# A two-layer SCNN on one core: x kept by channel and half, first weights placed by TensorE, first coefficients in PSUM, products for four rows, and a column scan fed from SBUF

## The chip, the core and the metric

The kernel runs on one core of a Trainium2 chip. The core has TensorE (PE: matrix products into PSUM), VectorE (DVE), ScalarE (ACT), GpSimd (POOL) and SyncE (SP), which mostly issues DMAs. SP, ScalarE and GpSimd each have a queue of DMAs. The metric is the device time of one execution in microseconds (us), as the median of several runs.

## The reference

x has the shape (32 images, 48 channels, 64 rows, 128 columns) in float32. Two layers, each with its own weights:

```python
x = x + _L0_conv_ref(_gn(x), ...)
x = x + _L1_conv_ref(_gn(x), ...)

# _gn: groupnorm, 16 groups of 3 channels; mean and variance per image and group
# inside _Ln_conv_ref; conv is a 1D convolution, 48 channels to 48, 5 taps
D[0] = x[0];   D[h] = x[h] + conv(D[h-1], down_w) + down_b      # rows, downwards
U[63] = D[63]; U[h] = D'[h] + conv(U[h+1], down_w) + down_b     # rows, upwards, same weights
R[0] = U[0];   R[v] = U[v] + conv(R[v-1], right_w) + right_b    # columns, to the right
L[127] = R[127]; L[v] = R[v] + conv(L[v+1], left_w) + left_b    # columns, to the left
```

The upward scan adds D of the row above the one that it makes (D' is D shifted by one row, the last one D[63]). Every row and every column depends on the one before it, so a layer has 2 x 63 row steps and 2 x 127 column steps in sequence. A row's convolution runs over its width, a column's over its height.

## The kernel before

**Phases.** The 32 images are four groups of 8. Twelve phases run one after the other (the table PHASES): a "rows" phase scans one group in one layer down and up (126 steps), a "cols" phase scans a pair of groups (two "halves") right and left (254 steps). The order is rows x0, rows x1, columns of this pair, rows x2, rows of layer 1's group 0, rows x3, columns of the second pair, rows of layer 1's groups 1 to 3, and the two column phases of layer 1. Two column phases (numbers 2 and 6 of the list, which starts at 0) come directly after the rows phase of their own second group; `follows` names them. They are called seams below.

**A step** (`step`, matmul L741, VectorE's scalar_tensor_tensor L750) makes one row or column. Channels and eight neighbouring positions lie on 3 x 128 partitions: 8 x 48 = 384, in three blocks, by the table PIECES (ten pieces: position e, channels c0 to c1, block o, first partition p0). The five taps with all neighbours become nine 128 x 128 x 128 float32 products (PRODUCTS), in the trace 18 matmul records, and three VectorE instructions add product, bias and the old row. In a rows phase the eight positions are e = w % 8, in a columns phase h % 8.

**SBUF.** One `arena` holds three slots and four stage units. A row image fills two slots, h below 32 in one, the rest in the other. A pair in column layout needs four quarters (`quarter`, 32 columns each, a slot each, so one is spilled to DRAM). `early` holds the weights down0, down1 and right (unused weight space serves as scratch at the start), then `last` and `junk`.

**DRAM copies.** `source[0]` (xin) is x in an order suited to both layouts: for each channel column position e, quarter, row and 32 values (4 columns of 8 images, "128-byte runs"). `source[1]` (mid) is the first layer's result, `ups` the result of the rows phases. `by_row`, `lines` and `by_col` are views of such a tensor: one for rows in row layout, one for rows as the input has them, one for columns.

**Input path.** `take_in` (L553) loads rows of x for the 8 images, partitions (channel, s) with s = 0 for h below 32 and 1 above. `permute` (L560, copies at L569) reorders one row pair (r and 32 + r) by four copies, `put_out` (L571) writes it to xin with two DMAs, one for each s, `move_rows` (L589) brings rows from DRAM into row layout by ten DMAs for eight rows, `scale_rows` (L606, ScalarE, L614) or `scale_at_once` (L618, L625) normalizes. The coefficients come from `scaling` (L312): an average over groups by a small product (L322), an expansion to row layout (L333), and a chain of small instructions on VectorE (L354 to L401; the groups' key is x0, x1, x2, x3, r0 to r3). With slack 0 they run on VectorE, otherwise partly on GpSimd.

**Order.** `at(t, fn, ...)` puts work on an agenda, t in steps; before each step everything due is emitted. `in_order` ties every instruction to the one before it on its engine, so each engine and DMA queue runs in program order.

**The start** (`first_group`, emitted as a whole ahead of the first step) handles group 0. It loads the x of 8 images in 16 DMAs (first all images' rows of `parts[0]`: r 0 to 15 with both s, then `parts[1]`: r 16 to 31) on SP. On ScalarE's queue `load_weights("down0")` copies the taps to DRAM and from there into the banded weight layout (5 + 25 DMAs), `load_constants` the masks and biases (2 + 10). VectorE takes the statistics (`InputStats`, L422, L425). `rows_by_product` makes rows 0 to 3 and 4 to 7 in row layout directly by TensorE products with identity pieces `to_row` (`make_ident`, L1074) and copies of PSUM by ScalarE (L1081), everything else goes through xin. Rows 0 to 3 are scaled by VectorE at once, the others in pieces of eight by ScalarE.

**A seam before.** The rows phase writes its rows to `upa` in pieces of eight, the last (first in h) in pieces of six and two; GpSimd's queue loads what the first quarter needs from there (`load_unit`, a a block of eight rows, e a row in it). `hold_queues` (L648) keeps SP's and ScalarE's next loads behind by a DMA to `pin` and a copy, each of which reads the second column of the first quarter; then follow the loads of quarter 1, alternating between SP and ScalarE.

Of the kernel before, what the change touches and what calls it, by code (L numbers as in the profile page):

```python
# [29 lines left out]
F32 = mybir.dt.float32  # L30
# [90 lines left out]
def kernel(  # L121
# [72 lines left out]
    source = [kept("xin"), kept("mid")]  # L194
# [9 lines left out]
    pin = dram.tile([FULL, 1], F32, tag="pin", name="pin")  # L204
# [9 lines left out]
    def by_row(t, e, h0, h1):  # L214


        t = t.rearrange("c (i q a e n) -> e a c i q n", i=E8, q=NQ, a=NH, e=E8)[e, h0 // E8]
        return t[:, h0 % E8 : h0 % E8 + h1 - h0].rearrange("c i q n -> c (i q) n")

    def lines(t, h0, h1):  # L220

        t = t.rearrange("c (i q a n) -> a c i q n", i=E8, q=NQ, a=NH)[h0 // E8]
        return t[:, h0 % E8 : h0 % E8 + h1 - h0].rearrange("c i q n -> c (i q) n")
# [9 lines left out]
    tail = {}  # L233

    def in_order(fn, *args):
# [5 lines left out]
        for ins in traced[n:]:  # L241
            if ins.engine in tail:
# [7 lines left out]
                )  # L250
            tail[ins.engine] = ins
# [29 lines left out]
    def load_constants(dma):  # L281
        for s in range(2):
            dma(sided(mask_sb)[s], mask[SIDES[s], SIDES[0]])
        for e, c0, c1, o, p0 in PIECES:
            dma(bd[p0 : p0 + c1 - c0, o], bias[c0:c1])
# [25 lines left out]
    def scaling(key, layer, g, averages, masks, slack=0):  # L311
# [5 lines left out]
        pool = nc.gpsimd if slack else nc.vector  # L317
# [25 lines left out]
        mean = small("mean")  # L343
        spare = small("dev")
        dev = spare[0 : FULL if n > 1 else PX, 0:n]
        if n > 1:
# [3 lines left out]
            expand(ps[:, 1 : 1 + NG], mean_c)  # L350
            yield
            nc.vector.tensor_tensor(dev, mean_p, ps[:, 1 : 1 + NG], ALU.subtract)
        else:
            nc.vector.tensor_tensor(dev, mean_p, ps[0:PX, 0:1], ALU.subtract)  # L354
        if n > 1:
            nc.vector.tensor_copy(mean, ps[:, 1 : 1 + NG])
# [6 lines left out]
        if n == 1:  # L363
            expand(ps[:, 2 + NG :], dev[:, 0])
        else:
# [5 lines left out]
            expand(ps[:, 2 + NG :], var_c)  # L371
        yield
        var = small("var")
        nc.vector.tensor_scalar(var, ps[:, 2 + NG :], GN_EPS, None, ALU.add)

        std = small("std")
        nc.scalar.activation(std, var, AF.Sqrt)
        if n == 1:
            expand(ps[:, 1 : 1 + NG], mean_p[:, 0])
        yield  # L380
        if n == 1:
            nc.vector.tensor_copy(mean, ps[:, 1 : 1 + NG])
        yield
        for _ in range(slack):
# [4 lines left out]
        pool.tensor_tensor(t0, var, r0, ALU.mult)  # L389
# [3 lines left out]
        scale, offset = (  # L393
            stat_pool.tile(
                [FULL, NG, GB], F32, tag=f"{t}{layer}{g}", name=f"{t}{layer}{g}"
            )
            for t in ("scale", "offset")
        )
        pool.tensor_tensor(scale, r0, t0, ALU.mult)
        pool.tensor_tensor(offset, mean, scale, ALU.mult)  # L400
        pool.tensor_scalar(offset, offset, -1.0, None, ALU.mult)  # L401
        coeffs[layer, g] = scale, offset
# [168 lines left out]
    def put_out(g, r, perm):  # L571


        n = perm.shape[-1] // (W * GB)
        for s in range(2):
            h = s * HALF + r
            dma(
                lines(source[0][g], h, h + n),
                sided(perm)[s].rearrange("p (m n) -> p m n", n=LINE),
            )  # L580
# [8 lines left out]
    def move_rows(k, h0, h1, to_dram):  # L589
# [4 lines left out]
        for h in range(h0, h1, E8):  # L594
            end = min(h1, h + E8)
            for o in range(NG):
                for e, c0, c1, p0 in pieces(o):
                    here = view[p0 : p0 + c1 - c0, o, h % HALF : h % HALF + end - h]
                    here = here.rearrange("p h (q n) -> p (h q) n", q=NQ)
                    there = by_row(t, e, h, end)[c0:c1]  # L600
# [25 lines left out]


# [20 lines left out]
    def hold_queues(k):  # L648

        done = quarter(k, 0)[:, 0, 0, RUN : RUN + 1]  # L650
        dma(pin, done)
        nc.scalar.copy(junk[:, BN - 1 :], done)
# [10 lines left out]
    def load_residual(k, j, i, nat):  # L663
# [3 lines left out]
        for e, c0, c1, p0 in pieces(o):  # L667
            dma(nat[p0 : p0 + c1 - c0], by_col(t, e, j)[c0:c1], nc.scalar if layer else None)
# [184 lines left out]
    def plan_rows(k, t0, prev):  # L853
# [13 lines left out]
        if following and follows(k + 1):  # L867
            cuts = [0, E8 // 4] + cuts[1:]
# [19 lines left out]
    def plan_cols(k, t0, prev):  # L888
# [3 lines left out]
        if follows(k):  # L892
            at(t0 + 1.2, hold_queues, k)
        for i in range(n):
            if follows(k) and UNITS[i][1] == 1:
# [4 lines left out]
                at(t0 - 1.5, load_unit, k, 0, i, 0, 1, E8 // 4, E8, other)  # L900
                at(t0, load_unit, k, 0, i, 0, 1, 0, E8 // 4, other)
# [3 lines left out]
            if follows(k):  # L905
                queue = nc.scalar if i % 2 else nc.sync
# [117 lines left out]
    def first_group():  # L1024
# [7 lines left out]

        def make_ident():
            for m, (e, c0, c1, o, p0) in zip(to_row, PIECES):
# [11 lines left out]
        rows = HALF // 2  # L1046
        parts = [wide_nat(SLOT + i * 2 * HALF * N * 2, rows) for i in range(2)]
        stats = InputStats("x0", GB)
        n = W * GB
# [10 lines left out]
        def permute_rows(i, r0, r1, ring, *engines):  # L1060
            for r in range(r0, r1):
                permute(parts[i], r, ring[r % len(ring)], engines)

        def put_rows(i, r0, r1, ring):
            for r in range(r0, r1):
                put_out(0, i * rows + r, ring[r % len(ring)])
# [18 lines left out]

        for i in range(2):
            for b in range(GB):
                take_in(0, i * rows, parts[i], slice(b, b + 1))
        nc.vector.memset(spare["right"], 0.0)
        nc.vector.memset(spare["left"], 0.0)  # L1090
        load_weights("down0", 0, DOWN, aside)
        load_constants(aside)
        make_ident()
        for b in range(GB):
            stats.take(0, parts[0], b)
        permute_rows(0, 8, 12, free, nc.gpsimd, nc.scalar)
        put_rows(0, 8, 12, free)
        rows_by_product(0, 4)
        spread_masks()
        permute_rows(0, 12, 15, free, nc.gpsimd, nc.scalar)  # L1100
        put_rows(0, 12, 15, free)
# [107 lines left out]
```

## Time and profile before

| what | us |
|---|---|
| median of 3 runs | 4292.32 (4289.52 to 4297.63) |
| profiled execution, device time | 4290.3 |
| its span, first to last instruction | 4288.2 |
| eight rows phases, 8 x 126 steps | 63 upward steps took 124.59 (from 526.61) |
| four columns phases, 4 x 254 steps | 127 leftward steps took 248.45 (from 2193.80) |
| last step to the end | from 4207.7 to 4288.2 |

The span is what the page and the trace count in; the device time lies 2.1 us above it. Times in the views are counted from the first instruction. A row of a timeline is: start, duration, engine, line, operation, what is written and what read, shape, count, and in brackets the idle time before it with what ended it. "PEld" is TensorE's loading of weights, which runs beside its products. A line name such as step_01u is the step's PSUM tile: layer 0, group 1, up. DMAs all have line L231, a helper's, and are told apart by what they write and read.

### The profile page before, as it was taken

What the parts mean: (1) busy time and instruction counts of PE and PEld (TensorE: products, weight loads), DVE (VectorE), ACT (ScalarE), POOL (GpSimd) and SP (SyncE); (2) the same over time, 40 slices, a digit from 0 to 9 for tenths busy, and PEclk for the clock granted to TensorE, in tenths of its full rate; (3) what the DMA queues carried; (4) which work ended last, traced back from release to release, by engine and by line L of the source; (5) the groups of instructions that cost most, each with busy time, mean ns of one, the idle gap of its engine ahead of it and who ended that gap; (6) DMA issues with size and microseconds to landing.
All of it is one profiled execution on the core that took longest, in us unless ns stands there. A gap on an engine that the chain in (4) does not pass through costs nothing. (4 is left out here: it accounts for less than half of the span.)

```text
span 4288.2 us, 89979 instructions
## 1 busy us (share of the span) xinstructions
PE 4058.9 (95%) x36648; PEld 4029.3 (94%) x36648; DVE 2164.5 (50%) x6503; ACT 1340.1 (31%) x2662; POOL 886.2 (21%) x906
## 2 busy tenths in 40 slices
PE   3699998999999999998999999999999999999992
PEld 1699998999999999998999999999999999999992
DVE  6345444446664444444446654444444444444443
ACT  1584301435793564100006772613000002210122
POOL 4271001325323020010005310000000024510352
PEclk9899999999999999999999999999999999999996
DMA  9599799857998979679308979939289049999999
GB/s 213 113 216 162 105 167 168 245 127 213 230 198 156 163 140 160 103 127 206 85 1 242 222 154 149 148 50 161 43 140 200 1 78 247 247 243 156 180 202 182
DMA packets 2116733, 680.12 MB, mean 159 GB/s; under 512 B 2005440, under 2 KB 2056160, under 8 KB 2076384
## 3 DMA queue, kind: packets, MB, share of 16 engines
q1 hardware_dynamic: 2015904, 581.64, 70.2%
q10 hardware_dynamic: 97216, 86.44, 9.9%
q0 software_dynamic: 3200, 6.30, 0.5%
q8 instruction: 288, 4.72, 0.5%
q14 instruction: 125, 1.02, 0.1%
HBM read 397.38 MB, written 295.98 MB: 162 GB/s over the span
## 5 line engine op out<-in xcount | busy, mean ns | idle before, releaser
L614 ACT ACTIVATE arena<-arena,offset,scale 128x256 f32<-128x256 f32 (+2 forms) x816 | 575.6, 801 | 432.9 <-DMA arena<-mid 176.1
L673 POOL TENSOR_TENSOR arena<-arena 128x2048 f32<-128x2048 f32 x80 | 363.1, 4553 | 1386.0 <-PE step_10l L741 434.1
L569 POOL COPY arena<-arena 96x256 f32<-96x256 f32 x448 | 265.0, 650 | 553.8 <-DMA arena<-in_x 444.2
L512 ACT ACTIVATE early<-arena 128x256 f32<-128x256 f32 x192 | 129.4, 674 | 477.2 <-POOL arena L673 471.2
L741 PE MATMUL step_00r<-arena,early 128*128 128x128 f32 x2286 | 251.5, 274 | 14.1 <-DMA arena<-upa 14.1
L741 PEld LDWEIGHTS step_00r<-arena,early 128*128 128x128 f32 x2286 | 251.1, 185 | 14.5 <-issue 14.4
L741 PE MATMUL step_01r<-arena,early 128*128 128x128 f32 x2286 | 250.6, 273 | 14.4 <-DMA arena<-upa 14.4
L741 PEld LDWEIGHTS step_01r<-arena,early 128*128 128x128 f32 x2286 | 250.4, 185 | 14.6 <-issue 14.5
L741 PE MATMUL step_11r<-arena,early 128*128 128x128 f32 x2286 | 251.3, 273 | 8.2 <-DVE arena L750 8.2
L741 PEld LDWEIGHTS step_11r<-arena,early 128*128 128x128 f32 x2286 | 250.8, 185 | 8.7 <-DVE arena L750 8.6
L741 PE MATMUL step_00l<-arena,wleft 128*128 128x128 f32 x2286 | 249.1, 272 | 0.0
L741 PEld LDWEIGHTS step_00l<-arena,wleft 128*128 128x128 f32 x2286 | 248.6, 184 | 0.0
L741 PE MATMUL step_10l<-arena,wleft 128*128 128x128 f32 x2286 | 248.5, 272 | 0.0
L741 PE MATMUL step_11l<-arena,wleft 128*128 128x128 f32 x2286 | 248.5, 272 | 0.0
L741 PE MATMUL step_01l<-arena,wleft 128*128 128x128 f32 x2286 | 248.4, 272 | 0.0
L741 PE MATMUL step_10r<-arena,early 128*128 128x128 f32 x2286 | 248.4, 272 | 0.0
L741 PEld LDWEIGHTS step_10l<-arena,wleft 128*128 128x128 f32 x2286 | 248.4, 184 | 0.0
L741 PEld LDWEIGHTS step_11l<-arena,wleft 128*128 128x128 f32 x2286 | 248.4, 184 | 0.0
L741 PEld LDWEIGHTS step_01l<-arena,wleft 128*128 128x128 f32 x2286 | 248.4, 184 | 0.0
L741 PEld LDWEIGHTS step_10r<-arena,early 128*128 128x128 f32 x2286 | 248.4, 184 | 0.0
L698 ACT COPY arena<-arena 128x256 f32<-128x256 f32 x172 | 99.7, 656 | 411.5 <-POOL arena L673 162.2
L240 ACT COPY early<-arena 128x1 f32<-128x1 f32 x2 | 0.4, 191 | 657.9 <-DVE arena L750 657.9
(189 smaller groups left out, 7171.3 us busy)
## 6 DMA issues: line engine op xcount, KB each, us to landing
arena<-in_x SPq DMA_DIRECT2D x24, 1536.0 KB, 11.6
xin<-arena SPq DMA_DIRECT2D x96, 384.0 KB, 4.7
arena<-xin SPq DMA_DIRECT2D x96, 384.0 KB, 8.5
mid<-arena SPq DMA_DIRECT2D x96, 384.0 KB, 7.8
arena<-mid SPq DMA_DIRECT2D x192, 192.0 KB, 4.2
upb<-arena SPq DMA_DIRECT2D x192, 192.0 KB, 3.9
arena<-upb SPq DMA_DIRECT2D x96, 384.0 KB, 12.3
arena<-xin SPq DMA_DIRECT2D x186, 192.0 KB, 4.3
```

The source lines that it names most:

```text
L240: fn(*args)
L512: nc.scalar.activation(junk[:, 0:n], view[:, b], AF.Identity, accum_out=self.sum[:, i, j : j + 1])
L569: copy(dst[:, r, q], src[:, r0 + r, q])
L614: nc.scalar.activation(args[0], args[0], AF.Identity, bias=args[2], scale=args[1])
L673: eng.tensor_tensor(unit, unit, nat, ALU.add)
L698: copy(by_w(perm)[:, a], src[:, a])
L741: nc.tensor.matmul(part(whole(ps[o])[0:m], -s), weights[:, i, at : at + m], part(src(i), s), start=seen[o] == 1, stop=seen[o] == left[o],)
```

## The change

- **x in DRAM.** Each group's xin is one tensor of 96 partitions (channel, s) with half the rows each. `put_out` is one DMA of all 96 partitions. The views are `x_by_row`, `x_by_col` and a changed `lines`; the residual loads of layer 0 read two runs of 4 KB where they read one of 8 KB.
- **First weights.** `load_kernel` fetches the five taps and the bias with six DMAs, on SP and ScalarE's queue alternately; `place_kernel` spreads them with 37 products of the identity pieces, into PSUM, and six ScalarE copies. `load_constants` shrinks to `load_masks` (2 DMAs). ScalarE's square root table is loaded at the start by a dummy instruction.
- **First coefficients.** With slack 0 (x0, x1, x3) `scaling` keeps variance, mean and one difference in the PSUM tile, so that its two-tensor instructions read one operand from PSUM.
- **Products make four rows.** `rows_by_product(4, 4)` is gone; rows 4 to 7 go through xin. `put_rows` now permutes and writes row by row, one engine for a row. `scale_first` scales rows 0 to 3 image by image: 15 VectorE instructions and 9 ScalarE instructions on 128 x 64 in place of four VectorE instructions.
- **Seams.** `send_row` copies the columns of quarter 0 in the first block of eight rows directly from row layout in SBUF to column layout in SBUF, in runs of 32 values: for e 0 to 3 row by row as the scan makes rows 7 to 0 (47 DMAs), then `send_rest` for e 4 to 7 (47), alternating between ScalarE's queue and SP. Rows 0 to 15 go to `upa` by quarters (`move_rows` with q): quarter 0 of rows 8 to 15 eight steps before the end, the others after it. GpSimd's loads of rows 0 to 7 are gone. `hold_queue` keeps only the ScalarE copy, without the DMA to `pin`; quarter 1 is loaded for half 1 on SP and half 0 on ScalarE's queue.

```diff
+    source = [
+        [
+            dram.tile([PX, MOIETY], F32, tag=f"xin{g}", name=f"xin{g}")[:, 0 : CHANNEL // 2]
+            for g in range(NGRP)
+        ],
+        kept("mid"),
+    ]
...
+    def x_by_row(t, e, h0, h1):
+        s, h = divmod(h0, HALF)
+        t = t.rearrange("(c s) (i q a e n) -> s e a c i q n", s=2, i=E8, q=NQ, a=NH // 2, e=E8)
+        t = t[s, e, h // E8, :, h % E8 : h % E8 + h1 - h0]
+        return t.rearrange("c i q n -> c (i q) n")
+
+    def x_by_col(t, e, j):
+        return t.rearrange("(c s) (i q n) -> i q c s n", s=2, i=E8, q=NQ)[e, j]
...
+            if ins.engine in queues and "DMA" in ins.opcode:
+                if fn in together and "queue" in tail:
...
+                        reason="together",
+                    )
+                tail["queue"] = ins
...
+        if not slack:
+            far = ps[0:PX, 1 + NG : 2 + NG]
+            nc.vector.tensor_tensor(far, mean_p, ps[0:PX, 0:1], ALU.subtract)
+            nc.vector.tensor_tensor(dev, mean_p, ps[0:PX, 0:1], ALU.subtract)
+            nc.vector.tensor_tensor(far, far, dev, ALU.mult)
+            nc.vector.tensor_tensor(dev, far, var_p, ALU.add)
+            yield
+            expand(var, dev[:, 0])
+            yield
+            nc.vector.tensor_scalar(var, var, GN_EPS, None, ALU.add)
+            r0 = small("std")
+            nc.scalar.activation(r0, var, AF.Sqrt)
+            expand(mean, mean_p[:, 0])
+            yield
+            yield
+            nc.vector.reciprocal(r0, r0)
+            nc.vector.tensor_tensor(var, var, r0, ALU.mult)
+            nc.vector.tensor_tensor(var, var, r0, ALU.mult)
+            nc.vector.tensor_scalar(var, var, -0.5, 1.5, ALU.mult, ALU.add)
+            nc.vector.tensor_tensor(scale, var, r0, ALU.mult)
+            nc.vector.tensor_tensor(offset, mean, scale, ALU.mult)
+            nc.vector.tensor_scalar(offset, offset, -1.0, None, ALU.mult)
+            return
...
-        for s in range(2):
-            h = s * HALF + r
-            dma(
-                lines(source[0][g], h, h + n),
-                sided(perm)[s].rearrange("p (m n) -> p m n", n=LINE),
-            )
+        dma(lines(source[0][g], r, r + n), perm.rearrange("p (m n) -> p m n", n=LINE))
...
+    def scale_first(k, h1, split):
...
+        for b in range(GB):
+            for o in range(NG):
+                it = view[:, o, b]
+                by, on = scale[:, o, b : b + 1], offset[:, o, b : b + 1]
+                if b < split:
+                    nc.vector.tensor_scalar(it, it, by, on, ALU.mult, ALU.add)
+                else:
+                    nc.scalar.activation(it, it, AF.Identity, bias=on, scale=by)
...
-    def hold_queues(k):
-        done = quarter(k, 0)[:, 0, 0, RUN : RUN + 1]
-        dma(pin, done)
-        nc.scalar.copy(junk[:, BN - 1 :], done)
+    def send_row(k, h, wanted):
+        here = row(k - 1, h)
+        for e, c0, c1, o, p0 in PIECES:
+            if e not in wanted:
+                continue
+            for i, d0, d1, to, q0 in PIECES:
+                a, b = max(c0, d0), min(c1, d1)
+                if i != h or a >= b:
+                    continue
+                turns[0] += 1
+                dma(
+                    quarter(k, 0)[q0 + a - d0 : q0 + b - d0, 1, to, e * RUN : (e + 1) * RUN],
+                    here[p0 + a - c0 : p0 + b - c0, o, 0:RUN],
+                    nc.scalar if turns[0] % 2 else nc.sync,
+                )
+
+    def send_rest(k, wanted):
+        for e in wanted:
+            for h in range(E8 - 1, -1, -1):
+                send_row(k, h, (e,))
...
+    def hold_queue(k):
+        nc.scalar.copy(junk[:, BN - 1 :], quarter(k, 0)[:, 0, 0, RUN : RUN + 1])
...
-            cuts = [0, E8 // 4] + cuts[1:]
+        seam = following and follows(k + 1)
+        if seam:
+            cuts = cuts[2:]
+            end = t0 + 2 * (H - 1)
+            at(end - E8, move_rows, k, E8, 2 * E8, True, 0)
+            for h in range(E8 - 1, -1, -1):
+                at(end - h, send_row, k + 1, h, range(0, E8 // 2))
+            at(end, send_rest, k + 1, range(E8 // 2, E8))
+            for q in range(1, NQ):
+                at(end + 0.1 if q == 1 else end + 1.6, move_rows, k, 0, 2 * E8, True, q)
...
-                at(t0 - 1.5, load_unit, k, 0, i, 0, 1, E8 // 4, E8, other)
-                at(t0, load_unit, k, 0, i, 0, 1, 0, E8 // 4, other)
...
-                queue = nc.scalar if i % 2 else nc.sync
+                queue = nc.sync if UNITS[i][1] else nc.scalar
...
+        def load_kernel():
+            nc.vector.memset(kernel, 0.0)
+            for j in range(TAPS):
+                d, si = divmod(TAPS - 1 - j, 2)
+                to = sided(kernel)[0][:, j * C : (j + 1) * C]
+                dma(to, w[SIDES[si], 0, DOWN, d, SIDES[0]], nc.scalar if j % 2 else nc.sync)
+            aside(sided(kernel)[0][:, TAPS * C :], bias[0:C].rearrange("c l k -> c (l k)"))
...
+        def place_kernel():
+            for i in range(NG):
+                ps = ps_rows.tile([FULL, BN], F32, tag=f"rows{i}", name=f"rows{i}")
+                todo = [(to_row[0], zeros, slice(0, NG * FULL + 6))]
...
+                for j, (lhs, rhs, to) in enumerate(todo):
+                    nc.tensor.matmul(
+                        ps[:, to], lhs, rhs, start=j == 0, stop=j == len(todo) - 1
+                    )
+                nc.scalar.copy(wt["down0"][:, i], ps[:, 0 : NG * FULL])
+                nc.scalar.copy(
+                    bd[:, i].rearrange("p l k -> p (l k)"), ps[:, NG * FULL :][:, 0:6]
+                )
...
-        load_weights("down0", 0, DOWN, aside)
-        load_constants(aside)
+        load_kernel()
...
+        place_kernel()
+        spread_masks()
         for b in range(GB):
             stats.take(0, parts[0], b)
...
+        put_rows(0, 4, 8, free, pool, act)
         rows_by_product(0, 4)
...
+        put_rows(0, 8, 14, free, pool, act)
+        put_rows(0, 14, 16, free, pool)
+        move_rows(0, 4, 8, False)
+        move_rows(0, 8, 16, False)
         for b in range(GB):
             stats.take(NBN // 2, parts[1], b)
             stats.aggregate(b)
...
-        scale_at_once(0, 0, 1, nc.vector)
-        scale_at_once(0, 1, 4, nc.vector)
+        scale_first(0, 4, 5)
         scale_rows(0, 4, 8)
         scale_rows(0, 8, 16)
+        put_rows(1, 0, 8, free, pool)
         move_rows(0, 16, 24, False)
         scale_rows(0, 16, 24)
...
+        put_rows(1, 8, 16, late, pool)
         move_rows(0, 24, 32, False)
         scale_rows(0, 24, 32)
...
+        put_rows(0, 0, 4, later, pool)
+        move_rows(0, 32, 40, False)
         scale_rows(0, 32, 40)
+        move_rows(0, 40, 64, False)
         take_in(1, 0, nats1[0])
```

## The prediction

> **What bounds the kernel now.** I read the page first, then the waits of TensorE, then its timeline, and for each long gap the timeline of the engine that ended it.
>
> ```profile
> span 4288.2 us, 89979 instructions
> PE 4058.9 (95%) x36648; PEld 4029.3 (94%) x36648; DVE 2164.5 (50%) x6503; ACT 1340.1 (31%) x2662; POOL 886.2 (21%) x906
> PE   3699998999999999998999999999999999999992
> ```
>
> TensorE is busy 95% of the span. The third line shows where it is not: the first four slices (107 us each), a dip in slices 7 and 19, and the last slice.
>
> ```profile
> PE rows L1074 <- DMA arena<-in_x: 41.7, 1, 41.7
> PE step_00d L741 <- DVE arena L750: 31.7, 6, 14.9
> PE step_00d L741 <- DVE arena L625: 24.7, 1, 24.7
> PE step_01r L741 <- DMA arena<-upa: 14.4, 1, 14.4
> PE step_00r L741 <- DMA arena<-upa: 14.1, 1, 14.1
> ```
>
> The columns are total, count and longest. The change can reach two places: the start, and the two seams (row scan to column scan) in slices 7 and 19. The timeline of TensorE (start, us) at the start:
>
> ```profile
> 60.01 16.57 PE L1074 MATMUL rows<-arena,early 96*128 96x512 f32 x18
> 78.22 0.35 PE L322 MATMUL ps_x<-mv_x_x,mask_x 96*96 96x8 f32 x2
> 107.83 17.66 PE L741 MATMUL step_00d<-arena,early 128*128 128x128 f32 x144 [24.72 <-DVE arena L625]
> 175.60 0.79 PE L741 MATMUL step_00d<-arena,early 128*128 128x128 f32 x2 [13.62 <-DVE arena L750]
> 208.63 0.80 PE L741 MATMUL step_00d<-arena,early 128*128 128x128 f32 x2 [14.85 <-DVE arena L750]
> ```
>
> The first step begins at 107.83, and row 32 is reached at 208.63. An unhindered step is 1.978 us (63 row steps in 124.6 us), so the 31 steps to there are 61.3 us; the other 39.5 of that 100.8 us are stalls at rows 8, 24 and 32. Behind the first step stands one VectorE line:
>
> ```profile
> 83.25 0.29 DVE L387 RECIPROCAL std_x<-std_x 128x24 f32<-128x24 f32 x1
> 83.58 22.07 DVE L389 TENSOR_TENSOR dev_x<-var_x,std_x 128x24 f32<-128x24 f32 x1
> 105.68 0.18 DVE L390 TENSOR_TENSOR dev_x<-dev_x,std_x 128x24 f32<-128x24 f32 x1
> ```
>
> L389 and L390 are alike, 22.07 against 0.18 us. GpSimd's row copies run back to back from 75.72 to 105.60 in its timeline, and L389 ends as they end. Behind rows 24 and 32 stands the SP queue:
>
> ```profile
> 104.68 1.31 SPq L231 DMA_DIRECT2D xin<-wleft x2
> 140.84 3.83 SPq L231 DMA_DIRECT2D xin<-arena x6
> ```
>
> SP waits 34.8 us here for ScalarE's L614 (the scaling of rows), so put-outs and moves of the later rows all start late.
>
> **What the Trainium skill says.** (1) "SBUF — State Buffer", section "Who interferes with whom": a VectorE instruction with two SBUF inputs contends with a GpSimd instruction that reads SBUF, the loser is blocked entirely; with at most one SBUF input, outside the two-port modes, it does not contend. The trace agrees once (L389); seven other two-input instructions that met these copies waited at most 0.4 us, so it is a risk per instruction, not a price. (2) "VectorE: DVE Perf Modes", section "Why PSUM operands drop a tier": an operand in PSUM rules the two-port mode out. No instruction of before tests this against a copy. (3) "DMA: Bandwidth & Descriptors", section "Queues, rings and completion order": each engine consumes descriptors in ring order. Agrees: put-outs issued by SP from 44.74 landed only from 66.69 on, 0.5 us apart, right behind the last x load (66.29). (4) "TensorE: Matmul & The Clock Gate", section "What's actually happening": after an idle window of about 3.4 us the clock is halved, until about as much busy time. In the windows view the clock around the seam (652 to 670) is 0.55, so I add 2.4 us to each long stall.
>
> **Loads and statistics.** The 25 weight DMAs and 10 bias DMAs on ScalarE's queue (16.52 and 8.90 us) go. SP's waits up to 260 us show that its x loads stood behind them (total, count, longest):
>
> ```profile
> SPq L231 <- DMA early<-taps: 11.9, 3, 6.2
> SPq L231 <- DMA bd<-in_b: 10.0, 2, 7.7
> SPq L231 <- DMA taps<-in_w: 8.2, 1, 8.2
> ```
>
> So the first eight loads land 5 to 6 us apart, the eighth at 41.57, and the later ones 3.0 apart. Now three tap DMAs of SP stand ahead (about 0.6 us each), the first load lands at about 8, the eighth at 8 + 7 x 3.0 = 29, the sixteenth at 53 to 54 instead of 66.29. VectorE's statistics take 2.47 + 0.37 us per load, less than the gap, so they end at 57. Placing the weights by TensorE is 37 small products and six copies, before the eighth load, in TensorE's empty 41.7 us: nothing. One product instead of two (18.6 us) ends near 48, ahead of 57; before, the second held the averages to 78.22. Averages: 57.3 instead of 78.22, -21 us.
>
> **First coefficients.** From 78.22 to the last coefficient is 28.5 us, of which L389 is 22. With PSUM operands no tensor-by-tensor instruction has two SBUF inputs, so no wait of that kind is left; one more VectorE instruction is 0.2, and the PSUM tile makes the expansion wait for ScalarE's square root (0.6; the table is loaded earlier, -1.3). 28.5 - 22 = 6.5: coefficients at 64. In place of four VectorE instructions (4.1 us) come 15 VectorE (0.2 to 0.55 each; not in before at this shape, the small TENSOR_SCALAR rows are 0.17 to 0.28) and 9 ScalarE (0.395 each, 3.6 us). They are single-source in SBUF, so they may meet copies: below 3 us alone, 22 more if starved. I take 5: first step at 69.5, -38.
>
> **Rows after the first four.** Rows 4 to 7 now go through DRAM. Twelve put-outs queue behind the loads; a row is 1.0 us of transfer, so the ring of seven buffers turns over from 54; the last copies end at about 63. Then ten moves (8.7 us for eight rows, 6 to 8.7 here) and 3.1 us to land: 73 to 75. ScalarE's 24 scalings x 0.395 = 9.5 end at 83.5. The scan needs row 4 at 69.5 + 3 x 1.978 = 75.4: stall 8 + 2.4. Rows 8 to 15: 24 x 0.508 = 12.2 more, 95.7 against a need of 93.8: 2. After that each eight rows cost GpSimd 19 us of copies (2.36 a row), SP 5 of put-outs (one 0.6 us issue for a row instead of two) and 9 of moves, and ScalarE 12.2, against 15.8 of scan. Copies from 63 on end at 82 and 101 (rows 16 to 23, 24 to 31), their put-outs at 86 and 102, moves land at 98.5 and 114.5, scalings end at 110.7 and 126.7, against needs of 111.5 and 127.3. Rows 32 to 39 need only four more copies: 139 against 143. I found no wait of these put-outs for ScalarE, which removes the 34.8 us. These margins are thin: I add 4 us. Sum of stalls 16.4 against 39.5. Row 32 at 69.5 + 61.3 + 16.4 = 147.2 instead of 208.63: -61; rounded to -60, since group 1's loads must come as much earlier (SP reaches them at some 160 instead of 225.30, -65, so they do).
>
> **Seams.** A column step is 248.45 / 127 = 1.956. From the last row step to the end of the right scan there are 265.5 us at the first seam (651.2 to 916.7) and 265.0 at the second: 16.8 over 248.4. Now 94 DMAs of 128-byte runs go from SBUF to SBUF, 47 on each of the two queues: 23.5 while the last eight rows are made, 2.5 of them after the last row, and 23.5 behind. With c us per DMA on a queue, the last column of the first eight lands 0.35 + 26c + 2.0 us after the scan (small DMAs at the seam land after 1.9 to 2.5) and is needed six steps (11.7) after the first. Excess: 26c - 9.4 + 2.4 of clock, at c = 0.57 (put-out issues measure 0.55 to 0.6) 7.8. Ten moves precede on SP (6 us), which I charge 0.7. So 8.5 instead of 16.8, twice: -17. At c = 0.5 it is -20. Above c = 0.67 the queues lag behind the rows already (2.94 sends on each in 1.978 us), all 47 run from seven rows (13.8 us) before the end, and the excess becomes 47c - 20.8: at 0.8 the gain is 0. The quarter's other columns come as whole rows behind these sends, some 15 steps ahead of their use.
>
> **Rest.** x1's and x3's scaling wait for a square root, 0.6 each: +1. One put-out for two on a queue, 4 KB runs for 8 KB in the residual loads: beside an engine-bound scan, 0. The tail (80 us from 4207.7) isn't touched. Sum on the profiled run's own 4290.3 (span 4288.2): 4290.3 - 60 - 17 + 1 = 4214. The median of the runs is 2.0 above the profiled one: 4216.
>
> **The rivals.** (a) VectorE's scale instructions starve as L389 did, or the loads stay 5.7 us apart because another queue's DMAs hold the semaphores. For: L389 itself; against: 30 fewer DMAs between. Coefficients at 76 to 86 instead of 64; but rows 16 to 40 are set by SP and ScalarE with some slack, so of 12 to 22 us only 10 to 15 show: 4228. (b) The seam gives nothing (c near 0.8; weight DMAs took 16.52 / 25 = 0.66, bias DMAs 0.89): 4233. (c) The other side: the sends choke the seam, because two queues carry 94 tiny DMAs while the DMA share there is 0.95 (640 to 652). Excess 47c - 20.8 must exceed 16.8 by 30 on each seam to eat the start's gain: c above 1.43. At 1.6 it is 54, and the time 4292 + 2 x 37.6 - 59 = 4308. (d) It doesn't do what it says: a put-out still waits for ScalarE or for a buffer, and row 32 keeps its 34.8 us wait in part: row 32 at 175, 4244.
>
> **How the numbers follow.** Forecast 0.58, (a) 0.17, (b) 0.13, (d) 0.06, (c) 0.05, and 0.01 that gains and losses cancel. Forecast's own range: first step 67 to 73, stalls 12 to 20, seam -10 to -24: 4200 to 4230. To hold 8 in 10 it has to reach (a) and (b), and 4195 below for a seam that hides entirely: 4196 to 4242. A change under 0.2% (8.6 us) can't be told from none. Faster 0.94, same 0.01, slower 0.05.
>
> **What would show it.** Right: the first step near 69, a stall of about 10 at row 4 and none above 4 after it, no tensor-by-tensor instruction above 1 us before it, the sixteenth x load at 54, row 32 near 147; at each seam a first wait below 5 us, small waits within eight steps. Wrong: a VectorE scale of over 5 us, SP waiting for L614, a stall at rows 16 to 32 above 5, queue spacings above 0.8 us at a seam, or a wait of the columns on later loads.

## Result and the profile after

The changed kernel takes 4239.2 us (median of 4 runs, 4236.2 to 4246.9) against 4290.9 before (4 runs, 4278.9 to 4297.6): ratio 0.9881, 95% interval 0.9867 to 0.9895. Predicted were 4216, in a range of 4196 to 4242. So it is faster by 52 us instead of the 76 forecast: inside the stated range, near its upper end, and outside the forecast's own range of 4200 to 4230.

The profiled execution is the slowest of the four: its span is 4245.1 us, 43.1 below that of before. First the page's head with TensorE's busy tenths in 40 slices. Of the low slices of before (3 and 6 at the start, 8 in slices 7 and 19) a 6 at the start is left, and an 8 is new in slice 8, in the right scan. Then TensorE's waits (total, count, longest):

```profile
span 4245.1 us, 90421 instructions
PE   6999999899999999999999999999999999999992
```

```profile
PE step_00d L837 <- DVE arena L846: 12.4, 7, 6.6
PE step_00r L837 <- DVE arena L846: 11.2, 1, 11.2
PE step_00d L837 <- DVE arena L690: 6.9, 2, 6.5
PE step_00r L837 <- DMA arena<-arena: 6.0, 1, 6.0
PE step_01r L837 <- DMA arena<-arena: 5.8, 2, 5.0
```

Where 31.7 and 24.7 us of waiting stood at the start there are 12.4 and 6.9, and the seams' first waits are 6.0 and 5.0 instead of 14.1 and 14.4. But step_00r, the right scan behind the first seam, has a wait of 11.2 that wasn't there before. The timeline of TensorE shows where these lie; the last row of the fence is VectorE's, in the wait of 11.2:

```profile
70.83 0.77 PE L837 MATMUL step_00d<-arena,early 128*128 128x128 f32 x2 [6.53 <-DVE arena L690]
...
120.22 0.80 PE L837 MATMUL step_00d<-arena,early 128*128 128x128 f32 x2 [6.60 <-DVE arena L846]
...
605.71 16.98 PE L837 MATMUL step_00r<-arena,early 128*128 128x128 f32 x126 [6.05 <-DMA arena<-arena]
624.34 174.52 PE L837 MATMUL step_00r<-arena,early 128*128 128x128 f32 x1604 [1.65 <-DMA upa<-arena]
810.09 62.14 PE L837 MATMUL step_00r<-arena,early 128*128 128x128 f32 x556 [11.23 <-DVE arena L846]
...
809.68 0.61 DVE L846 SCALAR_TENSOR_TENSOR arena<-step_00r,bd,arena 128x128 f32<-128x128 f32 x2 [11.55 <-DMA arena<-upa]
```

The first step begins at 70.83 instead of 107.83. In step_00r, 126 + 1604 matmuls of 18 a step are 96 steps: the scan stops where quarter 3 begins, because VectorE waits for a load of it. From the first matmul of each phase in both traces:

| stage | before | after | difference |
|---|---|---|---|
| to the first step of x1 (step_01d) | 400.8 | 350.5 | -50.3 |
| first seam: upward scan x1 and right scan | 390.1 | 397.0 | +6.9 |
| second seam: upward scan x3 and right scan | 389.5 | 387.2 | -2.3 |
| step_02d, rows behind the first columns phase | 127.1 | 134.1 | +7.0 |
| all else | | | -4.4 |

Of "all else", 3.2 lie in the last right scan, step_11r. It takes 256.2 us here and 255.5 to 260.2 in the other traces, so this isn't to be put down to the change.

A seam's two scans without any wait are 124.5 + 248.3 = 372.8 us; what is above that I call its excess: 17.3 and 16.7 before, 24.2 and 14.4 after.

So the start gains 50 of the 60 us forecast, and the seams give nothing: 38.6 us of excess after, 34.0 before, 17 forecast. Two questions are left: what eats the seams' gain, and which part of the change made the start's.

### The profile page after: what moved, and what is told of

It reads as the page before. It is cut to its first block, busy times and chain, and to the rows that moved or that the text cites. A ratio compares the mean times of both kernels' runs of the same rounds, so it can differ in the third digit from the quotient of the medians.

```text
span 4245.1 us, 90421 instructions
## 1 busy us (share of the span) xinstructions
PE 4072.4 (96%) x36704; PEld 4050.5 (95%) x36704; DVE 2142.6 (50%) x6517; ACT 1346.5 (32%) x2680; POOL 870.8 (21%) x879
## 5 line engine op out<-in xcount | busy, mean ns | idle before, releaser
L837 PE MATMUL step_00r<-arena,early 128*128 128x128 f32 x2286 | 253.6, 275 | 18.9 <-DVE arena L846 11.2
```

The lines of the kernel that those rows point to most:

```text
L837: nc.tensor.matmul(part(whole(ps[o])[0:m], -s), weights[:, i, at : at + m], part(src(i), s), start=seen[o] == 1, stop=seen[o] == left[o],)
```

## Experiments

All but experiment 9 start from the changed kernel; a diff shows what differs, with "..." for lines left out. "Step 33" is the first matmul of step 33 of the first phase: 208.6 before, 160.4 after, and 157.7 to 159.5 in experiments 1 to 4, which have the same start (first step at 69.0 to 70.8). Experiments 5 to 8 and 10 are one execution each. Since executions of the changed kernel alone spread from 4236 to 4248, these five are read by their stages more than by their one time.

**1. The changed kernel again.**

> The changed kernel a second time, unaltered. In its profile the first seam's right scan stood 11.2 us at column 97, waiting for the last loads of quarter 3, which landed 203.6 us after the first column step (166.9 before the change). Theory S (SP's order: 60 moves to DRAM that used to lie ahead of the column scan now lie in SP's queue between quarter 0 and the loads of quarters 1 to 3): the loads land again near 200 us after the first column step, and a stall of 3 to 15 us is there again. Theory N (the stall belongs to that one execution, whose time was 4246.9 against 4236 to 4242 of the others): no stall, and the right scan of the first seam takes about 251 us.

4246.2 us (ratio to before 0.9885, 0.9855 to 0.9915). The stall is there again, 6.3 us at the same step:

```profile
812.19 63.14 PE L837 MATMUL step_00r<-arena,early 128*128 128x128 f32 x556 [6.33 <-DVE arena L846]
```

The excess is 23.2 at the first seam and 9.4 at the second. It isn't one execution's accident: the stall stands in all seven traces that keep these seams (the two, and experiments 5 to 8 and 10), with 3.5 to 15.0 us.

**2. The seams of before.**

```diff
-            cuts = cuts[2:]
...
-            at(end, send_rest, k + 1, range(E8 // 2, E8))
...
+            cuts = [0, E8 // 4] + cuts[1:]
...
+                at(t0 - 1.5, load_unit, k, 0, i, 0, 1, E8 // 4, E8, other)
+                at(t0, load_unit, k, 0, i, 0, 1, 0, E8 // 4, other)
```

> The changed kernel with the seams of the kernel before: rows to DRAM in pieces, GpSimd loads the first quarter, both queues held. Only the start is then changed. From the end of the row scan to the end of the right scan 265.5 us at the first seam (272.4 in the profile of the changed kernel), 265.0 at the second (262.6). My forecast of the new seams was -8.3 each, so by it this kernel is 17 us slower than the changed one. Theory S: the new seams are worth -3 to -5 each at their beginning, and +11 at column 97 of the first, so this kernel is between 8 us slower and 5 us faster.

4234.2 us (0.9864, 0.9837 to 0.9890), 12 below the changed kernel beside it. The intervals overlap, so it isn't shown to be faster, but it isn't 17 us slower, as my forecast wanted. Excess 17.9 and 17.2, no stall at quarter 3:

```profile
612.04 251.62 PE L840 MATMUL step_00r<-arena,early 128*128 128x128 f32 x2286 [14.61 <-DMA arena<-upa]
```

The old seam pays 14.6 us once and then nothing. The new one pays it in pieces. The two excesses of a kernel sum to 34 to 35 us in the three traces with the old seams (before, this one and experiment 9) and to 33 to 41 in the seven with the new ones. As a part of the change the seams are worth nothing.

**3. Moves of quarters 1 to 3 by GpSimd's queue.**

```diff
-                at(end + 0.1 if q == 1 else end + 1.6, move_rows, k, 0, 2 * E8, True, q)
+                at(end + 0.1, move_rows, k, 0, 2 * E8, True, q, nc.gpsimd)
```

> The changed kernel, but the 60 moves of quarters 1 to 3 of rows 0 to 15 to DRAM are issued by GpSimd's queue right behind the row scan, in place of SP's behind its sends. Theory S (order of SP): quarter 1's loads start 15 to 20 us earlier, quarter 3's last load lands 20 to 35 us earlier (near 170 us after the first column step), no stall at column 97, first seam 261 us, time 5 to 11 us below the changed kernel. Rival B (the 16 DMA engines are full from 625 to 800, share 0.92 to 1.04, so that it doesn't matter who issues): quarter 3 lands within 5 us of where it was, the stall stays.

4237.2 us (0.9868, 0.9845 to 0.9891), 9.0 below the changed kernel beside it (the intervals overlap). The stall at quarter 3 is gone, and the first seam's excess falls from 24.2 to 11.5:

```profile
604.22 16.40 PE L837 MATMUL step_00r<-arena,early 128*128 128x128 f32 x126 [6.79 <-DMA arena<-arena]
622.38 234.90 PE L837 MATMUL step_00r<-arena,early 128*128 128x128 f32 x2160 [1.76 <-DVE arena L846]
```

The bytes are the same, and only the issuing queue differs, with the time of the issue, so SP's order set the stall (theory S), not the DMA engines (rival B). SP's queue in the changed kernel behind the first row scan shows it (start, duration, count):

```profile
589.15 31.23 SPq L250 DMA_DIRECT2D arena<-arena  x47
620.42 15.74 SPq L250 DMA_DIRECT2D upa<-arena  x20
641.04 12.15 SPq L250 DMA_DIRECT2D arena<-upa  x10
653.24 28.55 SPq L250 DMA_DIRECT2D upa<-arena  x40
```

Before the change 30 moves of whole rows did this work, and SP had issued them by 659.6, ahead of the columns (665.3). Now sixty moves of quarters (upa<-arena) take 44 us of SP behind the sends, and the later loads on SP come late: the last of quarter 3 lands 203.6 us after the first column step instead of 166.9 (175.1 in this experiment). At the second seam it is late too, 154.6 instead of 118.3, but there that is still ahead of its use, 96 column steps or 187.8 us after the first.

The second seam's excess is 17.3 here, though: the last send on SP landed 6.0 us after its issue (mean 2.4), and the scan waited 4.4 us for it. The second seam with sends on two queues varies, from 9.4 to 17.3 in eight traces.

**4. Sends on three queues.** As experiment 3, and:

```diff
-                    nc.scalar if turns[0] % 2 else nc.sync,
+                    (nc.scalar, nc.sync, nc.gpsimd)[turns[0] % 3],
```

> As the kernel with the moves on GpSimd's queue, and the 94 sends alternate over three queues, ScalarE's, SP's and GpSimd's, 31 or 32 on each. In the changed kernel a send takes 0.64 us of a queue, the last lands 24.1 us after the row scan, and the excess of a seam over its column steps is 12.7 and 14.1 us (without the stall at column 97). If a queue's issue paces them: the last send lands 14 us after the row scan and the excess falls to 6 or 7 on each seam, 6 to 7 us less than the kernel with two queues. If the DMA engines or the landing pace them: no change. If GpSimd's sends are dearer than 1 us: the excess grows.

4220.8 us (0.9831, 0.9808 to 0.9854). Excess 6.5 and 7.0:

```profile
603.66 250.32 PE L837 MATMUL step_00r<-arena,early 128*128 128x128 f32 x2286 [4.55 <-DMA arena<-arena]
```

The last send lands 15.2 us after the row scan's end instead of 24.1. With two queues a send follows the last on its queue after 0.67 to 0.71 us, with three after 0.72 to 0.79 (behind the row scan after 0.70 to 0.74 on SP's and ScalarE's, 0.50 on GpSimd's), so 94 of them pass at 0.34 and some 0.27 us each. The queues' issue paces them, as supposed; the DMA share in the changed kernel in this stretch is at most 0.28.

**5. Coefficients in SBUF.**

```diff
-        if not slack:
+        if False:
...
-        pool = nc.gpsimd
+        pool = nc.gpsimd if slack else nc.vector
```

> The changed kernel with the coefficients of x0, x1 and x3 worked out in SBUF again, as before. Before the change one VectorE instruction of this chain (two SBUF inputs) took 22.07 us beside GpSimd's copies; now these copies run from 58.4 to 65.5 and the chain from 60.0 to 65.6. Forecast's theory (two SBUF inputs can be blocked by a GpSimd copy, PSUM operands can't): a tensor-by-tensor instruction of this chain waits until the copies pause, at most to about 66, so one of 1 to 6 us shows and the first step comes 1 to 5 us later than 70.8 (69.3 in the repeat). Rival (the 22 us were a single accident): all of them below 0.6 us, first step within 1.5 us. Step 33 (160.4 and 158.1) moves by at most 2, since rows 16 to 31 hold the scan.

First step 71.6, step 33 at 161.1, one time of 4240.2. Nothing is blocked; of the chain's rows:

```profile
59.23 0.49 DVE L417 TENSOR_TENSOR dev_x<-dev_x 96x8 f32<-96x8 f32 x1
59.76 0.62 DVE L419 TENSOR_TENSOR dev_x<-dev_x,mv_x_x 96x8 f32<-96x8 f32 x1
...
64.13 0.28 DVE L448 TENSOR_TENSOR dev_x<-var_x,std_x 128x24 f32<-128x24 f32 x1
```

So in this execution the PSUM coefficients are worth nothing at the start, and my expectation of 1 to 5 us fell. It doesn't show that such instructions can't be held: the copies pause from 64.36 to 66.73 here, L448 began 0.23 us ahead of that, and the rest of the chain ran in the pause.

**6. Weights by 40 DMAs.**

```diff
-        load_kernel()
...
-                if (i, b) == (0, 2):
-                    load_masks(aside)
...
+        load_weights("down0", 0, DOWN, aside)
+        load_masks(aside)
+        for e, c0, c1, o, p0 in PIECES:
+            aside(bd[p0 : p0 + c1 - c0, o], bias[c0:c1])
...
-        place_kernel()
```

> The changed kernel with the first weights and biases by 40 DMAs on ScalarE's queue as before, no placing by TensorE. Forecast's theory (these DMAs hold up the x loads): the x loads land up to 6 us apart again, the eighth near 41 instead of 31, the sixteenth at 62 to 67 instead of 56.4, the first step 6 to 10 us later, near 79, step 33 6 to 10 us later. Rival (the loads are paced by bandwidth alone): the sixteenth load at 56 to 58, first step within 2 us.

The eighth load lands at 38.2 instead of 31.0, the sixteenth at 64.3 instead of 56.4, first step 78.8, step 33 at 169.2, one time of 4262.9. As forecast: against the five traces with the start of the change this part is worth 8 to 10 us at the first step and 9 to 12 at step 33.

**7. Products for eight rows.**

```diff
-        put_rows(0, 4, 8, free, pool, act)
         rows_by_product(0, 4)
...
-        move_rows(0, 4, 8, False)
+        rows_by_product(4, 4)
...
-        put_rows(0, 0, 4, later, pool)
+        put_rows(0, 0, 8, later, pool)
```

> The changed kernel with two products, rows 0 to 7, as before; rows 4 to 7 don't go through DRAM before they are needed. The averages stand behind the second product on TensorE: it ends 18.6 us after the first, near 68 instead of 49.6, so the first step comes 8 us later, near 78; ScalarE then scales rows 4 to 7 without waiting for moves, and the wait at row 4 goes. If GpSimd's and SP's chain of the rows 16 to 31 sets the rest, as I now think, step 17 is 0 to 6 us earlier than 120.2 (eight put-outs and ten moves fewer ahead of it) and step 33 within 4 us of 160. If ScalarE sets it, step 33 is 8 us later.

First step 99.1, not 78; step 33 at 170.3; one time of 4263.5. On VectorE:

```profile
73.53 0.18 DVE L403 TENSOR_TENSOR offset<-ps_x,scale 128x24 f32<-128x24 f32 x1
73.75 21.92 DVE L404 TENSOR_SCALAR offset<-offset 128x24 f32<-128x24 f32 x1
95.70 3.79 DVE L690 TENSOR_SCALAR arena<-arena,scale,offset 128x64 f32<-128x64 f32 x15
```

and on GpSimd, the rows before and after the end of that wait:

```profile
84.11 6.94 POOL L621 COPY arena<-arena 96x256 f32<-96x256 f32 x12
90.98 4.65 POOL L621 COPY early<-arena 96x256 f32<-96x256 f32 x8
100.07 2.39 POOL L621 COPY wleft<-arena 96x256 f32<-96x256 f32 x4 [4.44 <-DMA xin<-wleft]
```

The wait of before is back, at another instruction. L404 has a single input, in SBUF, and is held until GpSimd's unbroken copies end at 95.63. The ten instructions ahead of it with an operand in PSUM took 0.16 to 0.19 each, beside the same copies. The reciprocal among them (L398), which reads SBUF alone, took 0.30 and wasn't held either.

**8. Two put-outs for a row pair.**

```diff
-        dma(lines(source[0][g], r, r + n), perm.rearrange("p (m n) -> p m n", n=LINE))
+        for s in range(2):
+            dma(
+                lines(sided(source[0][g])[s], r, r + n),
+                sided(perm)[s].rearrange("p (m n) -> p m n", n=LINE),
+            )
```

> The changed kernel with two put-outs for a row pair again, one for each half, on the new layout of x in DRAM. Each costs SP 0.6 us more. If SP's queue sets when rows 16 to 31 come (put-outs of eight rows, 4.8 us more, ahead of each ten moves): steps 17, 25 and 33 start 4 to 5, 8 to 10 and up to 14 us later. If GpSimd's copies (2.4 us a row) set them: all within 3 us.

Steps 17, 25 and 33 start at 130.9, 166.6 and 193.8 instead of 120.2, 141.2 and 160.4; one time of 4290.1, nearly the whole gain of the change. The first step, too, comes at 77.0 instead of 70.8. It isn't the 0.6 us a piece. The waits of SP from 60 to 175 us, here and (second fence) in the changed kernel:

```profile
SPq L250 <- ACT arena L671: 34.6, 3, 12.5
```

```profile
SPq L250 <- DMA xin<-arena: 6.8, 4, 3.3
```

A put-out of a half reads every second partition of its buffer, and is made to wait for ScalarE's scaling (L671) of other rows in the arena: the scaling of rows 8 to 15 ends at 96.65, and the put-outs, whose buffers lie in the place of rows 16 to 31, go on at 96.71. One of all 96 partitions isn't made to wait. That the split brings the wait is shown; that it comes from the bookkeeping of strided reads in the framework is only my reading.

**9. The kernel before with the new layout and the single put-out alone.**

The edit to the kernel before is the change's own, its first part and nothing else:

```diff
-        for s in range(2):
...
+        dma(lines(source[0][g], r, r + n), perm.rearrange("p (m n) -> p m n", n=LINE))
```

> The kernel before with the first part of the change alone: x in DRAM by channel and half, one put-out for a row pair, and the views that go with it. Undoing the single put-out in the changed kernel cost 33 us at step 33 (193.8 against 160.4), with SP waiting 34.6 us for ScalarE's scalings. If this wait is what the half-wise put-outs bring (theory): in the waits of SP none for L614's counterpart above 2 us, steps 25 and 33 no longer 13 to 15 us late, step 33 at 175 to 185 instead of 208.6, time 24 to 34 us below the kernel before. Rival (the parts only pay together, since the first step at 107.8 stays): the first step stays at 107 or later and step 33 moves by less than 12. Also: whether the 22 us of one VectorE instruction beside GpSimd's copies come again (then the first step is at 105 to 110), or were an accident (then at 84 to 88).

4258.4 us (0.9913, 0.9896 to 0.9930), 36.7 below the kernel before beside it, of the 52 that the whole change gains. First step 108.3, as before, but step 25 at 162.5 and step 33 at 178.3 instead of 208.6: 30 us from this part alone. Of SP's waits for ScalarE's scaling none is left; in the kernel before they were (60 to 235 us):

```profile
SPq L231 <- ACT arena L614: 44.5, 2, 34.8
```

And the blocked instruction is at the same place again (the line that was L389), so it is no accident of one execution:

```profile
83.17 0.29 DVE L405 RECIPROCAL std_x<-std_x 128x24 f32<-128x24 f32 x1
83.49 22.65 DVE L407 TENSOR_TENSOR dev_x<-var_x,std_x 128x24 f32<-128x24 f32 x1
```

Its step_02d takes 131.9 us (127.1 before), without any change at the seams.

**10. Eight rows by products, and no VectorE instruction that reads only SBUF.** As experiment 7, and:

```diff
-            nc.vector.tensor_tensor(offset, mean, scale, ALU.mult)
-            nc.vector.tensor_scalar(offset, offset, -1.0, None, ALU.mult)
+            nc.vector.scalar_tensor_tensor(offset, mean, -1.0, scale, ALU.mult, ALU.mult)
...
-        scale_first(0, 4, 5)
+        scale_first(0, 4, 0)
```

> The changed kernel with products for eight rows (first step at 99.1, one VectorE instruction with a single SBUF input blocked for 21.92 us), and in it no VectorE instruction between the averages and the first step that has all its inputs in SBUF, the reciprocal apart: the negation of the offset is merged into a product with an operand in PSUM, and rows 0 to 3 are scaled by ScalarE's 24 instructions (9.5 us) instead of 15 on VectorE and 9 on ScalarE. Theory (GpSimd's unbroken copies block VectorE instructions that read only SBUF, and don't block those with an operand in PSUM): nothing above 0.6 us, coefficients near 74, first step at 84 to 86 although the copies run on to 95. Rival (any VectorE instruction can be caught): one instruction of 15 us or more again, first step near 99 or later.

First step 81.8, step 33 at 155.3, one time of 4233.1. GpSimd copies without a break from 62.9 to 95.5, and nothing on VectorE is held:

```profile
72.56 0.18 DVE L402 TENSOR_TENSOR scale<-ps_x,std_x 128x24 f32<-128x24 f32 x1
72.78 0.18 DVE L403 SCALAR_TENSOR_TENSOR offset<-ps_x,scale 128x24 f32<-128x24 f32 x1
84.78 0.76 DVE L845 SCALAR_TENSOR_TENSOR arena<-step_00d,bd,arena 128x128 f32<-128x128 f32 x2 [11.82 <-PE step_00d L836]
```

The rival that an instruction is caught whatever it reads has VectorE's work from 84.8 to 95.5 against it: 15 instructions of the scan's first steps, with TensorE's product in PSUM among their inputs, ran beside the copies and took 0.34 to 0.35 each. Experiment 12 has the same start and shows the same. So the mechanism is the one forecast, but it lies in operands that the change had left in SBUF. And with it gone, eight rows by products are 2 to 5 us earlier at step 33 than four (157.7 to 160.4), although the first step is 11 later.

**11. Put-outs ahead of moves in SP's queue.** As experiment 4, and:

```diff
-        move_rows(0, 8, 16, False)
...
+        put_rows(1, 0, 4, free, pool)
+        move_rows(0, 8, 16, False)
         scale_rows(0, 8, 16)
-        put_rows(1, 0, 8, free, pool)
+        put_rows(1, 4, 8, free, pool)
```

> The kernel with sends on three queues and moves on GpSimd's (4220.8 us), and in its start SP issues the put-outs of rows 16 to 19 (and 48 to 51) ahead of the moves of rows 8 to 15 instead of behind them. In the changed kernel these moves (17.4 us for rows 4 to 15) stand ahead of the put-outs, GpSimd's ring of buffers runs full, and step 17 starts at 120.2 after a wait of 6.6. If SP's order sets rows 16 to 31: step 17 starts 4 to 6 us earlier (114 to 116), step 33 3 to 6 us earlier, time near 4216. If ScalarE sets them: step 9 gets later and step 17 stays within 1 us.

4223.3 us (0.9835, 0.9822 to 0.9848), not told from experiment 4. Step 9 at 103.1 instead of 95.4, step 17 at 121.9 instead of 120.0, step 33 at 162.8. A miss: the wait at row 16 (7.8 in experiment 4) is gone, but 9.5 us stand at row 8 (1.8 there) and 6.1 at row 24 (2.0). What SP gains for rows 16 it takes from rows 8.

**12. Experiments 4 and 10 together.**

> The changed kernel with what the runs so far gained: products for eight rows with no VectorE instruction that reads only SBUF before the first step (the reciprocal apart), and the sends on three queues with the moves of quarters 1 to 3 on GpSimd's. If the two gains add: first step near 82, step 33 near 155 (160.4 in the changed kernel), the two seams with 6 to 7 us of excess each (first 24, second 14 in the changed kernel), time 4220.8 - 4 = 4217, between 4212 and 4221. If the earlier start is lost again behind the first phase: 4220 to 4224, as with the three queues alone.

4219.1 us (0.9833, 0.9819 to 0.9846), runs from 4211 to 4228; step 33 at 155.7, excess 5.4 and 4.8, and a profiled span of 4209.3. Faster than both kernels, but not told from experiment 4 by its times.

## Why the prediction was right, and where it was off

- **Loads and statistics:** right. Sixteenth load at 56.4 (53 to 54 forecast), averages at 59.5 (57.3). Experiment 6 shows the worth of the new loading of weights, 8 to 10 us at the first step.
- **First coefficients:** right in time (first step 70.8, forecast 69.5), wrong in the reason. I took "L389 is 22" away because of the PSUM operands. Experiment 5 takes these back and nothing happens; experiment 7 keeps them and the 22 us come back. What removed them is timing, and so luck: the chain now ends at 65.6, beside a short run of copies (58.4 to 65.5) and ahead of the long one (67.6 to 84), mainly because the second product is gone. The Trainium skill's rule ("SBUF — State Buffer", section "Who interferes with whom") holds in experiments 7 and 10, but for the length: it has the loser blocked for one whole instruction of the other, and here the wait lasted over some 38 copies of 0.6 us. L404 fits its clause that single-source instructions contend in the two-port mode (no view shows the mode). I had priced that case for the 15 scale instructions ("22 more if starved"), not for L404. The scale instructions took 6.2 us where I had 5.
- **Rows after the first four:** stalls were to sum to 16.4 and row 32 to come at 147.2; it came at 160.4, 13.2 later. Of these 1.3 are the first step's, and 2.0 come from counting 31 steps where 32 lie between (so the stalls of before are 37.5, not 39.5). The other 9.9 are stalls: 89.6 us from step 1 to step 33, less 32 x 1.978, are 26.3. The waits themselves sum to 14.2, and I had 14 (8 at row 4, 2 at row 8, 4 as a margin), but they lie elsewhere: 3.0 at row 4, 1.7 at row 8, 6.6 at row 16, 2.9 at row 24. What I had too small is the term for slow steps behind a wait: 2.4, charged once, where 12.2 are left. From 84.8 to 96.8, 120.2 to 138.2 and 141.2 to 160.4, behind such waits, the granted clock is 0.86, 0.90 and 0.83. The wait at row 16 comes from the order of SP's queue, which I had at nothing: the put-outs of rows 16 to 23 stood behind 17.4 us of moves, and the next moves waited 3.7 us for these put-outs to land (experiment 11 shifts the wait to other rows, and wins nothing). My remark that no put-out waits for ScalarE was right, and the largest term of the change: 30 us alone (experiment 9), 33 when undone (experiment 8). I had not set its worth apart. Without it the rest of the new start is worth 15 us at step 33 (193.8 against 208.6), though its first step is 31 earlier.
- **Seams:** this step failed. The term "8.5 instead of 16.8, twice: -17" measured +6.9 and -2.3. First, c was 0.67 to 0.71, not 0.57, so the formula's branch for lagging queues (47c - 20.8) gives 10.7 to 12.6. Experiment 3's first seam has 11.5, but without the stall at quarter 3 the seams with two queues have 9.4 to 19.5 in all, a spread that the formula lacks. Second, the loads of quarters 1 to 3 behind sixty moves in SP's queue stood in the sum with nothing ("some 15 steps ahead of their use" speaks of the first quarter's columns); those of quarter 3 came 3.5 to 15.0 us too late at the first seam in all seven traces. "A wait of the columns on later loads" was on my list of signs, without a price.
- **Rest:** the residual loads in 4 KB runs were put at 0, but step_02d takes 7.0 us more here, 4.8 in experiment 9 and 1.8 to 9.1 in the other traces of the new layout (one trace of before). In the trace SP issues four of them in 3.8 to 4.0 us where it took 3.2 to 3.4 (3.2 and 3.8 in experiment 9). That is 1.2 of the 7.0, and ScalarE's scaling of rows 32 to 47 behind them had no time to spare. What makes the 7.0 stays open.

Of the rivals, (b), no gain at the seams and 4233, is nearest to what happened by its number; its reason, a c near 0.8, is not what was measured. (a), starving, was avoided by timing alone.

## What to carry to other kernels

A wait that disappears must be shown to disappear for the reason named: undo the part alone, since timing can hide it. When transfers move from ahead of a seam to behind it, follow the issuing queue to the last load that stands on it, not only to the next one. Price a wait of TensorE with the slow steps behind it: here 14.2 us of waits brought 12.2 more. And where a queue waits for an engine that its DMA has nothing to do with, the form of the DMA (which partitions it reads) may decide it.

## What the runs showed of the hardware

- A VectorE instruction that reads only SBUF can be held by GpSimd's copies not for one copy of 0.6 us but for as long as they follow each other: 22.07, 22.65 and 21.92 us in three kernels, with one input or two. Others of the same kind beside such copies took 0.22 to 0.79. So did the changed kernel's scale instructions (L690): 0.34 each on average while the copies pause (65.7 to 67.6), 0.63 beside them (67.7 to 71.8). Those with an operand in PSUM took 0.16 to 0.35 beside copies. Which one is caught stays open.
- A small SBUF-to-SBUF DMA costs SP's or ScalarE's queue 0.67 to 0.71 us in the changed kernel and lands about 2.1 us after its issue, at a DMA share of at most 0.28. A third queue, GpSimd's, issues one in 0.50 us behind the row scan (experiment 4), and from the first issue to the last 94 of them take 26.0 us instead of 31.7.
